# Two of 32 score maxima, the rounding of the maxima and the division of an attention kernel on GpSimd and ScalarE, with value products one step later

## The chip, the cores and the metric

The kernel runs on one core of a Trainium2 chip. The metric is device time in microseconds (us), from launch to end of one execution; lower is better. Engines: PE is TensorE's matmul, PEld its weight load, DVE is VectorE, ACT is ScalarE, POOL is GpSimd, SP is SyncE, which here only issues DMAs.

## What is computed

The program is a stack of four layers on x of shape (1, 2048, 128), all float32. Each layer is a feed-forward half, an attention, and the same feed-forward again; every part adds its result to x.

The four attentions are ordinary softmax attentions:

```
q, k, v = projections of layernorm(x)
s       = q k^T * scale            (per head; layers 0 and 3 causal)
p       = exp(s - rowmax(s))
out     = (p v) / rowsum(p)        (heads joined, output projection, added to x)
```

Layer 0 has 8 heads of 16 and is causal. Layers 1 and 2 have 16 heads of 8 and no mask. Layer 3 has 16 heads of 64 and is causal. The feed-forwards (mixtures of experts, a quantised one, a ternary one) are not touched by the change.

Any number close to the row maximum serves as well as the maximum itself, since it cancels between numerator and denominator; it only has to keep the exponential in range.

## The kernel before

Twelve stages follow one another: ffn0, attn0, ffn0, ffn1, attn1, ffn1 and so on. Stages overlap a little: while one ends, the next takes its first steps where its inputs are ready (the calls of `io.lead`).

The change lies in `flash`, the two-pass attention loop, and in `packed`, which feeds it for attn0, attn1 and attn2. In these, four heads form a group whose rows lie side by side in the partitions, so that four small matmuls run together in the PE array. An iteration `its[n]` is one group `g` and one block `qc` of 512 queries. attn1 and attn2 have four groups and four blocks, 16 iterations each; attn0 has two groups and four blocks.

Every iteration is done twice over its keys.

- Stream A (`stream_a`, `some`, `maxima`) is the first pass. For 128 queries (`r`), 512 keys (`kc`) and two heads (`j0`, `j0 + 1`), PE writes the scores of both heads into one PSUM tile of 2 x 512 columns (line 1071), and VectorE reduces it to two maxima in `mp` (line 1089). A non-causal iteration has 4 x 4 x 2 = 32 such tiles. They live in tag `s1`, which has two buffers. When all are done, `maxima` reduces `mp` over the key blocks to `mx` (line 1100), and `put_max` rounds it into a bf16 part (line 1556) and a bf16 remainder (line 1557) in `top`. Some time later `put` has PE add `top` to the queries by matmuls into `pm` (lines 1566 and 1570), and ScalarE copies that to `q2` (line 1574), so that the scores of the second pass come out with the maximum already subtracted.
- Stream B (`stream_b`) is the second pass. For each 128 keys (`kt`, 16 of them in a non-causal iteration) and each of the four heads, PE writes transposed scores of 128 keys x 512 queries into a bank of tag `s2`, which has three buffers (line 1213), and ScalarE takes the exponential into a tile `pt` (line 1222). `values` multiplies the four `pt` of a `kt` with v and adds them up in `pv`, of which there is one buffer (line 1159); it does so in two halves of the columns, one behind the second head and one behind the fourth head of the next `kt`.

After the last `kt`, `finish` has ScalarE copy `pv` to `ov` (line 1582). A little later `normal` has PE transpose it into an `s2` bank `po` (line 1587), VectorE takes the reciprocal of the row sums (line 1592) and multiplies (line 1593) into `os`. When a block has all its groups, `out_a` and `out_b` project it and add it to x.

PE's order is written out by hand: every matmul of the loop passes through `pe`, which keeps it in program order. The main loop of `flash` interleaves the streams: for the columns that B has emitted it asks how far A should be, runs A up to there, then takes one step of B. In the steady part this gives, per slot, one s2 score, one s1 tile, another s2 score and one half of a value product. Delayed pieces (`put`, `normal`, `out_a`) are queued by `after` with a delay in nanoseconds of an assumed PE clock. VectorE's and ScalarE's orders come from the scheduler, by readiness and priority, with some pairs tied by `in_order`.

In a causal iteration the tile on the diagonal is masked. In attn3 (`halved`), `half_masks` does this with four small bf16 matmuls that add a mask to the scores in PSUM (line 1026). In attn0 (`tiled and causal`) the mask was added by VectorE while it reduced: one `tensor_tensor_reduce` per head with a strip of zeros and minus infinity (line 1081), whose maximum is then read from an accumulator.

Of the kernel before, what the change touches and what calls it, by code (L numbers as in the profile page):

```python
# [17 lines left out]
P = 128  # L18
# [46 lines left out]
def tile_macaron(ctx: ExitStack, tc: tile.TileContext, a: dict, out: bass.AP, stages=STAGES):  # L65
# [32 lines left out]
    minus_half = const.tile([P, TC], F32, name="minus_half")  # L98
    nc.gpsimd.memset(minus_half, -0.5)

    def cs(name):
# [866 lines left out]
    OUT_A = 4000.0  # L968

    def flash(io, pool, early, its, nh, causal, scale, s1, s2, pv_mm, put_max, begin, finish, poll=None,
# [7 lines left out]

        halved = nh == 2
        clock = [0.0]
        total = [0]
        later = []
# [20 lines left out]

        if halved:

            halves = {}  # L1010
            for name in ("ident", "maskq", "maskk"):
                raw = pool().tile([P, 2, P], F32, name="halfraw", tag="halfraw", bufs=2)
                for j in range(2):
                    nc.sync.dma_start(
                        out=raw[P // 2 * j : P // 2 * (j + 1)],
                        in_=a["consts"][:, slice(*CONSTS[name])].rearrange("(b i) k -> i b k", b=2),
                    )
                halves[name] = pool().tile([P, 2, P], BF16, name="half" + name)
                nc.vector.tensor_copy(halves[name], raw)

        def half_masks(outs, mask):

            for b in range(2):
                for j in range(2):
# [3 lines left out]
                    ))  # L1028

        if tiled and causal:  # L1030
            junk = pool().tile([P, CH], F32, name="junk")
            strip = pool().tile([P, CH], F32, name="strip")
            nc.gpsimd.memset(strip[:, : CH - P], 0.0)
            nc.vector.tensor_copy(strip[:, CH - P :], cs("maskq"))

# [18 lines left out]
        def some(n, turns, mp):  # L1054

            g, qc = its[n]
            nk = chunks(qc)
            for first, (r, kcs) in enumerate(turns):
                before = hook(n, kcs[0], r) if hook is not None else None
                if first == 0 and before is None:  # L1060
                    before = newest[0]
                for kc in kcs:
                    for j0 in range(0, nh, 2):
                        ps = first_pass_bank()
                        last = causal and kc == qc
                        masked = last and not tiled
                        w = (r + 1) * P if last else CH
                        for j in range(2):
                            o = j * CH
                            lhsT, rhs = s1(n, j0 + j, r, kc)  # L1070
                            pe(nc.tensor.matmul(  # L1071
                                ps[:, o : o + w], lhsT, rhs[:, :w], start=True, stop=not masked
                            ))
                            pos[0] += w
                        if masked:
                            half_masks([ps[:, j * CH + w - P : j * CH + w] for j in range(2)], "maskq")
                        both = ps.rearrange("p (j n) -> p j n", j=2)
                        with tc.high_priority() if not waiting[0] else nullcontext():
                            if last and tiled:
                                for j in range(2):  # L1080
                                    ins = nc.vector.tensor_tensor_reduce(
                                        junk[:, :w], both[:, j, :w], strip[:, CH - w :], 1.0, NEG,
                                        ALU.add, ALU.max, mp[:, r, j0 + j, kc : kc + 1],
                                    )
                                    if before is not None:
                                        in_order(ins, before)
                                        before = None
                            else:
                                ins = nc.vector.tensor_reduce(  # L1089
                                    mp[:, r, j0 : j0 + 2, kc], both[:, :, :w], AX.X, ALU.max,  # L1090
                                )
                        if before is not None:
                            in_order(ins, before)
                            before = None
                        yield 2 * w if tiled else w

        def maxima(n, mp):
            nk = chunks(its[n][1])
            mx = pool().tile([P, TC, nh], F32, name="mx", tag="mxa", bufs=3)
            nc.vector.tensor_reduce(mx, mp[:, :, :, :nk], AX.X, ALU.max, negate=True)  # L1100
            put, newest[0] = put_max(n, mx, pe)

            def done():
                put()
                ready.add(n)

            after(2000.0, done)

        newest = [None]
        waiting = [False]  # L1110

# [15 lines left out]
        def stream_b():  # L1127
            pend = [None]

            def values(half=None):  # L1130

                if pend[0] is None:
                    return
                n, kt, nt, c0, pts, pv, last_exp = pend[0]
                if halved:
# [12 lines left out]
                if half == 0:  # L1148
                    pend_half[0] = 1
                    if hi == CH:  # L1150
                        pend[0] = None
                        pend_half[0] = 0
                else:
                    pend[0] = None
                for j in reversed(range(nh)):
# [21 lines left out]
            for n, (g, qc) in enumerate(its):  # L1177
# [3 lines left out]
                nt = chunks(qc) * TC  # L1181
                pv = None
                for kt in range(nt):
# [4 lines left out]
                    if halved:  # L1188
# [11 lines left out]
                        for j in range(2):  # L1200
                            pts[j] = early.tile([P, CH], F32, name="pt", tag="pt", bufs=2 * nh + 2)
                            ex = nc.scalar.activation(pts[j][:, c0:], outs[j][:, c0:], AF.Exp, scale=scale)  # L1202
                        step((CH - c0) * (len(terms[0]) - 2))
                        yield 2 * (CH - c0)
                        values()
                    for at_j, j in enumerate(() if halved else order):
                        if alive[0] or at_j % 2:
                            ps = bank("s2")
# [8 lines left out]
                        if diag and not tiled:  # L1217
                            pe(nc.tensor.matmul(
                                ps[:, c0 : c0 + P], masks_b["ident_b"], masks_b["maskk_b"], start=False, stop=True
                            ))  # L1220
                        pt = early.tile([P, CH], F32, name="pt", tag="pt", bufs=2 * nh + 2)
                        ex = nc.scalar.activation(pt[:, c0:], ps[:, c0:], AF.Exp, scale=scale)  # L1222
# [11 lines left out]
                        if tiled and alive[0]:  # L1234
                            if at_j % 2:
                                values(at_j // 2)
                        elif at_j == (split_at if alive[0] else nh - 1):
                            values()
                    if pv is None:
                        pv = held("pv")  # L1240
                    pend[0] = (n, kt, nt, c0, pts, pv, ex)
                    if not alive[0]:
                        io.lead(2.3)
                if poll is not None:
                    at[1] = nt
                    if flush and n + 1 < len(its) and its[n + 1][0] != g:
                        values()
                    poll(at)
            values()

# [70 lines left out]

    def attention_scratch(early):
        return lambda dt, name: early.tile([P, CH], dt, name=name, tag="pt", bufs=10)

    def packed(io, early, hd, causal, scale, project, w, wv, wo, bias=None, outs=True):
# [11 lines left out]
        wv, wo = w[:, wv : wv + C], w[:, wo : wo + C]  # L1337
        scratch = attention_scratch(early)
        vall = [early.tile([P, TC, C], F32, name=f"vall{c}") for c in range(NC)]
# [210 lines left out]

        def put_max(n, mx, pe):
            top = tops[n % 3]
            tv = top.rearrange("p a r (j s) -> p a r j s", s=span)[:, :, :, :, 3:8:4]
            for i in range(nq):
                m = mx[:, :, i * per : (i + 1) * per]
                nc.vector.tensor_copy(tv[:, i, :, :, 0], m)
                last = nc.vector.tensor_tensor(
                    tv[:, i, :, :, 1], m, tv[:, i, :, :, 0], ALU.subtract
                )

# [18 lines left out]
        def finish(n, pv, after, pe):  # L1579
# [4 lines left out]
            def normal():  # L1584
                ps = bank("po")
                for r in range(TC):
                    pe(nc.tensor.transpose(
                        ps[:, r * P : (r + 1) * P], ov[:, r * P : (r + 1) * P], ident
                    ))
                po = ps.rearrange("p (r j m) -> p r j m", r=TC, j=4)  # L1590
                rc = room[0].tile([P, TC, 4], F32, name="rc", tag="rc", bufs=2)
                nc.vector.reciprocal(rc, po[:, :, :, hd])
                nc.vector.tensor_tensor(
                    os[qc][:, :, g * 4 * hd : (g + 1) * 4 * hd].rearrange(
                        "p r (j d) -> p r j d", j=4
                    ),
                    po[:, :, :, :hd],
                    rc.unsqueeze(3).to_broadcast([P, TC, 4, hd]),
                    ALU.mult,
                )  # L1600
                if g == n_groups - 1:
                    after(OUT_A if causal else 1500.0, out_a)
# [61 lines left out]
        with tc.tile_pool(name="att", bufs=1) as pool, tc.tile_pool(name="far", bufs=1) as far:  # L1664
# [10 lines left out]
            room.append(pool)  # L1675
            room.append(far if causal else early if outs else pool)

# [712 lines left out]
```

## Time and profile before

| quantity | value |
|---|---|
| median of three runs | 3737.1 us (3736.11 to 3738.52) |
| the profiled execution, its own time | 3720.81 us |
| its span, first to last instruction | 3719.1 us |
| mean granted TensorE clock | 0.950 |
| busy in the span: PE, PEld | 3404.5 us (92%), 1837.3 us (49%) |
| DVE, ACT, POOL | 2853.9 us (77%), 2025.6 us (54%), 817.1 us (22%) |
| attn0, attn1, attn2, attn3, about | 178 to 450, 790 to 1490, 1650 to 2390, 2580 to 3540 us |
| line 1089, all forms | 1440 reduces, 1627.7 us busy |
| line 1222, all forms | 2368 exponentials, 1220.5 us busy |

How to read the profile: it is one execution, recorded by the hardware. A row of groups has the source line, the engine, the operation, the tiles written and read by their names in the program, their shapes, the count, then busy time in us, the mean of one in ns, and the idle time of the engine just before, with what ended it (`<-`). A row of the timeline has start and duration in us; `x7` are seven such instructions back to back, and a bracket is idle time before it. In a row of stretches, each engine has its busy us and its count of instructions. Durations of back-to-back instructions overlap a little, so a pitch, start to start, is the better measure of what one costs its engine. The tiles of both passes appear as `s`.

The times differ between stages: the shares over the whole span say little about attn1 and attn2, where VectorE and PE are busy 97% and more of most stretches.

### The profile page before, as it was taken

The numbers are of one execution on the slowest core, as the hardware profiler recorded it, in microseconds if no ns is written. First come the engines' busy times: TensorE is split into PE (matmuls) and PEld (weight loads), VectorE is DVE, ScalarE is ACT, GpSimd is POOL, SyncE is SP. The second block draws the span as 40 slices with busy tenths as digits, with TensorE's granted clock in tenths as the row PEclk, the third lists the DMA queues.
The fourth block names the chain that finished last, engine by engine and source line by source line (L and its number), as shares of the span: only waits on it lengthen the run. The fifth ranks groups of instructions, "written<-read, shape, count | busy, mean of one in ns | idle before, by whom it ended". The sixth has DMA issues, their size and how long they took to land. (4 is left out here: it accounts for less than half of the span.)

```text
span 3719.1 us, 64518 instructions
## 1 busy us (share of the span) xinstructions
PE 3404.5 (92%) x25325; PEld 1837.3 (49%) x25325; DVE 2853.9 (77%) x4729; ACT 2025.6 (54%) x3815; POOL 817.1 (22%) x816
## 2 busy tenths in 40 slices
PE   7689987989999999997999999898889999999989
PEld 5543366854333333883333333376444444445457
DVE  6588556778999995778999999544777877788852
ACT  3346722317888888333888888731333344444442
POOL 1511124000000000210000000232555445533341
PEclk9779989979999999996999999898999999999999
DMA  3420123000000000100000000012443232211010
GB/s 106 98 52 14 37 62 91 7 20 9 15 6 16 6 4 7 55 25 21 10 16 10 12 6 1 26 44 68 151 146 112 96 106 98 97 57 52 24 35 12
DMA packets 124977, 170.18 MB, mean 46 GB/s; under 512 B 25152, under 2 KB 52930, under 8 KB 124672
## 3 DMA queue, kind: packets, MB, share of 16 engines
q1 hardware_dynamic: 122112, 160.80, 13.8%
q0 software_dynamic: 2560, 5.25, 0.9%
q8 instruction: 199, 3.26, 0.4%
q14 instruction: 106, 0.87, 0.1%
HBM read 101.25 MB, written 45.87 MB: 40 GB/s over the span
## 5 line engine op out<-in xcount | busy, mean ns | idle before, releaser
L1089 DVE TENSOR_REDUCE mp<-s 128x2 f32<-128x1024 f32 (+3 forms) x1440 | 1627.7, 1183 | 80.2 <-PE s L1071 56.7
L1222 ACT ACTIVATE pt<-s 128x512 f32<-128x512 f32 (+1 forms) x2368 | 1220.5, 601 | 217.7 <-PE s L1213 165.2
L1213 PE MATMUL s<-q,km 32*128 32x512 f32 (+2 forms) x2368 | 735.0, 493 | 28.8 <-ACT pt L1222 18.6
L1159 PE MATMUL pv<-pt,v 128*32 128x256 f32 (+1 forms) x8568 | 732.2, 414 | 22.9 <-ACT ov L1582 11.2
L1071 PE MATMUL s<-km,qt 32*128 32x512 f32 (+3 forms) x2368 | 617.1, 506 | 64.9 <-DVE mp L1089 45.3
L1213 PEld LDWEIGHTS s<-q,km 32*128 32x128 f32 (+1 forms) x2368 | 323.9, 184 | 531.4 <-issue 339.5
L1202 ACT ACTIVATE pt<-s 128x512 f32<-128x512 f32 (+3 forms) x640 | 306.3, 530 | 361.3 <-PE s L1194 216.3
L143 POOL TENSOR_TENSOR rs<-rs,minus_half 128x4 f32<-128x4 f32 x56 | 57.3, 1023 | 1491.8 <-DVE rs L142 1468.1
L2071 DVE TENSOR_TENSOR sum<-sum,pt 128x512 f32<-128x512 f32 (+3 forms) x328 | 260.0, 808 | 86.9 <-ACT pt L1202 85.6
L1159 PEld LDWEIGHTS pv<-pt,v 128*32 128x32 f32 x8568 | 169.2, 108 | 317.7 <-issue 147.1
L1194 PE MATMUL s<-q,k 64*128 64x512 f32 (+3 forms) x1920 | 295.1, 400 | 14.9 <-ACT pt L1202 10.5
L1159 PE MATMUL pv<-pt,latv 128*64 128x512 f32 (+3 forms) x1280 | 307.5, 560 | 1.3 <-ACT pt L1202 1.3
L2071 POOL TENSOR_TENSOR sum<-sum,pt 128x512 f32<-128x512 f32 (+1 forms) x200 | 264.7, 1324 | 179.8 <-ACT pt L1202 176.4
L1071 PEld LDWEIGHTS s<-km,qt 32*128 32x128 f32 (+1 forms) x2368 | 236.2, 191 | 123.8 <-DVE mp L1089 82.3
L1194 PEld LDWEIGHTS s<-q,k 64*128 64x128 f32 x1920 | 159.1, 186 | 222.8 <-issue 140.5
L715 ACT ACTIVATE sg<-pg 128x1024 f32<-128x1024 f32 x72 | 74.0, 1027 | 158.2 <-PE pg L229 142.0
L1071 PE MATMUL s<-k,q 64*128 64x512 f32 (+3 forms) x640 | 131.9, 430 | 19.0 <-DVE mp L1089 18.8
L1873 DVE TENSOR_TENSOR rot<-rot,tab 128x512 f32<-128x512 f32 x128 | 87.8, 686 | 74.8 <-PE rot L229 43.3
L725 PEld LDWEIGHTS pd<-l1d,h 128*128 128x128 f32 x1152 | 139.0, 191 | 5.6
L725 PE MATMUL pd<-l1d,h 128*128 128x128 f32 x1152 | 139.8, 275 | 0.0
L717 DVE TENSOR_TENSOR h<-pu,sg 128x1024 f32<-128x1024 f32 x72 | 87.8, 1220 | 51.7 <-PE pu L229 46.5
L1888 ACT CAST h<-rot 128x512 fp32r<-128x512 f32 x64 | 39.6, 619 | 159.5 <-POOL rot L1883 159.5
(572 smaller groups left out, 4736.3 us busy)
## 6 DMA issues: line engine op xcount, KB each, us to landing
tab<-in_l3rope SPq DMA_DIRECT2D x66, 256.0 KB
q<-q SPq DMA_DIRECT2D x32, 512.0 KB
k<-k SPq DMA_DIRECT2D x32, 512.0 KB
l0e<-in_l0e SPq DMA_DIRECT2D x32, 256.0 KB
q<-h SPq DMA_DIRECT2D x32, 256.0 KB
q<-rot SPq DMA_DIRECT2D x32, 256.0 KB
k<-h SPq DMA_DIRECT2D x32, 256.0 KB
k<-rot SPq DMA_DIRECT2D x32, 256.0 KB
```

Source lines behind the costliest of these rows:

```text
L715: nc.scalar.activation(sg, pg, AF.Silu)
L717: nc.vector.tensor_tensor(h.rearrange("p m n -> p (m n)"), pu, sg, ALU.mult)
L725: nc.tensor.matmul(pd[:, i, :], h[:, m, i * P : (i + 1) * P], wd[:, m, :], start=m == 0, stop=m == 1,)
L1071: pe(nc.tensor.matmul(ps[:, o : o + w], lhsT, rhs[:, :w], start=True, stop=not masked))
L1089: ins = nc.vector.tensor_reduce(mp[:, r, j0 : j0 + 2, kc], both[:, :, :w], AX.X, ALU.max,)
L1159: i = pe(nc.tensor.matmul(pv[out_rows, lo:hi], lhsT, pts[j][:, lo:hi], start=kt == 0, stop=kt == nt - 1 and hi == CH))
L1194: pe(nc.tensor.matmul(outs[j][:, c0:], lhsT, rhs[:, c0:], start=i == 0, stop=i == len(terms[0]) - 1 and not diag,))
L1202: ex = nc.scalar.activation(pts[j][:, c0:], outs[j][:, c0:], AF.Exp, scale=scale)
L1213: pe(nc.tensor.matmul(ps[:, c0:], lhsT, rhs[:, c0:], start=i == 0, stop=i == len(terms) - 1 and (tiled or not diag),))
L1222: ex = nc.scalar.activation(pt[:, c0:], ps[:, c0:], AF.Exp, scale=scale)
L1873: nc.vector.tensor_tensor(t.bitcast(F32), ps, halves["tabs"][i], ALU.mult)
L2071: eng.tensor_tensor(t[:, c0:], other[:, c0:], pts[j][:, c0:], ALU.add)
```

## The change

The edits of `flash` and `packed`:

1. Two tiles aside. In attn1 and attn2 (`aside`), in every iteration but the first, the first-pass tiles (r, kc, j0) = (1, 0, 0) and (1, 2, 2), which are numbers 4 and 21 of 32 (counted from 0), are not reduced by VectorE. `halving` has ScalarE copy the tile to SBUF in two copies of 128 x 512, and GpSimd halve it three times: difference of two halves, maximum with zero, plus the second half. What is left, 2 x 64 columns, is reduced by VectorE in `maxima`, ordered behind the iteration's last plain reduce and ahead of `mx`.
2. Rounding. In the same iterations `put_max` runs its copy and subtraction on GpSimd, and `put` is due 3000 instead of 2000 behind them.
3. Division. In attn1 and attn2, but for the last iteration of each, `normal` has ScalarE copy `po` to `ot`, and GpSimd take the power -1 of the row sums and multiply.
4. Later values. In attn1 and attn2 (`lag`), `pend` is a list, and while stream A lives a value product is emitted half a `kt` later than before: its first half behind the fourth head of the next `kt`, its second half behind the second head of the one after. `pt` has 12 buffers instead of 10.
5. Causal masks. attn0 now masks by `half_masks` like attn3, and reduces masked tiles with the plain reduce; the strip and `tensor_tensor_reduce` are gone. `half_masks` needs two mask tables, loaded by four DMAs at the start of attn0.
6. `ov`, `ot` and `oT` of attn1 lie in another pool.

Counts of instructions, before and after: VectorE 128 masked reduces and 128 accumulator reads to none, plain reduces from PSUM 1440 to 1444, 60 small reduces of what GpSimd left, reciprocals of `po` 40 to 10, and 30 fewer each of the rounding's copy and subtraction and of the multiply in attn1 and attn2. ScalarE 150 more copies. GpSimd 660 more operations. PE 256 more mask matmuls, each with a weight load of its own.

```diff
+    ASIDE = ((1, 0, 0), (1, 2, 2))
...
+        lag = tiled and not causal
...
+        aside = tiled and not causal
...
-                        masked = last and not tiled
+                        masked = last
...
+                        if aside and n and (r, kc, j0) in ASIDE:
+                            halving(ps, mp[:, r, j0 : j0 + 2, kc])
+                            yield 2 * w
+                            continue
                         with tc.high_priority() if not waiting[0] else nullcontext():
-                            if last and tiled:
-                                for j in range(2):
-                                    ins = nc.vector.tensor_tensor_reduce(
-                                        junk[:, :w], both[:, j, :w], strip[:, CH - w :], 1.0, NEG,
-                                        ALU.add, ALU.max, mp[:, r, j0 + j, kc : kc + 1],
-                                    )
...
+                            ins = nc.vector.tensor_reduce(
+                                mp[:, r, j0 : j0 + 2, kc], both[:, :, :w], AX.X, ALU.max,
+                            )
+                            last_max[0] = ins
...
+        def halving(ps, out):
+
+            t = pool().tile([P, 2, CH], F32, name="copied", tag="copied", bufs=2)
+            d = pool().tile([P, 2, CH // 2], F32, name="over", tag="over", bufs=1)
+            for j in range(2):
+                nc.scalar.copy(t[:, j], ps[:, j * CH : (j + 1) * CH])
+            m = CH // 2
+            while m >= CH // 8:
+                nc.gpsimd.tensor_tensor(d[:, :, :m], t[:, :, :m], t[:, :, m : 2 * m], ALU.subtract)
+                nc.gpsimd.tensor_scalar_max(d[:, :, :m], d[:, :, :m], 0.0)
+                nc.gpsimd.tensor_tensor(t[:, :, :m], d[:, :, :m], t[:, :, m : 2 * m], ALU.add)
+                m //= 2
+            left.append((out, t[:, :, : 2 * m]))
...
         def maxima(n, mp):
             nk = chunks(its[n][1])
+            while left:
+                out, t = left.pop(0)
+                in_order(nc.vector.tensor_reduce(out, t, AX.X, ALU.max), last_max[0])
...
+            if aside and n:
+
+                put, _ = put_max(n, mx, pe, nc.gpsimd)
+            else:
+                put, newest[0] = put_max(n, mx, pe)
...
-            after(2000.0, done)
+            after(3000.0 if aside and n else 2000.0, done)
...
                         if tiled and alive[0]:
-                            if at_j % 2:
-                                values(at_j // 2)
+                            if at_j % 2 and (not lag or at_j == nh - 1 or len(pend) > 1):
+                                values(pend_half[0] if lag else at_j // 2)
...
+                if causal or n == len(its) - 1:
...
+                else:
+                    ot = room[1].tile([P, CH], F32, name="ot", tag="ov", bufs=2)
+                    nc.scalar.copy(ot, ps)
+                    po = ot.rearrange("p (r j m) -> p r j m", r=TC, j=4)
+                    rc = room[0].tile([P, TC, 4], F32, name="rc", tag="rc", bufs=2)
+                    nc.gpsimd.tensor_tensor(rc, po[:, :, :, hd], minus_one, ALU.pow)
+                    nc.gpsimd.tensor_tensor(
+                        out, po[:, :, :, :hd],
+                        rc.unsqueeze(3).to_broadcast([P, TC, 4, hd]), ALU.mult,
+                    )
```

## The prediction

> **What bounds the kernel now.** I read the page's 40 slices first, then the busy time of each engine by stretches of 100 us, then the groups, the waits and the timeline inside one attention stage. The slices show two long level stretches, 850 to 1440 and 1750 to 2350 us, the non-causal attentions attn1 and attn2, where nearly all of the change lies. From the stretches (us; then busy us of PE, PEld, DVE, ACT, POOL; granted clock):
>
> ```profile
> 1100.00:1200.00 100.00, 97.56 (x995) 37.49 (x987) 97.91 (x100) 88.35 (x171) 0.00 (x0) 1.00 0.05 13
> 1200.00:1300.00 100.00, 97.60 (x998) 37.76 (x994) 97.52 (x96) 88.51 (x172) 0.00 (x0) 1.00 0.03 8
> ```
>
> VectorE is full, GpSimd empty, ScalarE at 88%. VectorE's groups in 900 to 1350 us:
>
> ```profile
> L1089 DVE TENSOR_REDUCE mp<-s 128x2 f32<-128x1024 f32 x372 | 427.4, 1220 | 3.2 <-PE s L1071 1.7 <-PE s L1213 1.3
> L1593 DVE TENSOR_TENSOR o<-po,rc 128x128 f32<-128x128 f32 x11 | 3.2, 291 | 0.4
> L1592 DVE RECIPROCAL rc<-po 128x16 f32<-128x16 f32 x11 | 2.8, 255 | 5.5 <-PE po L1587 5.5
> L1557 DVE TENSOR_TENSOR top<-mx,top 128x16 bf16<-128x16 f32 x11 | 2.5, 232 | 0.4
> ```
>
> The maxima are nearly all of it. Starts of the mx reduce give an iteration: (1352.55 - 886.12)/12 = 38.87 us for 32 maxima, 64 exponentials and 64 value products. The timeline gives the rules by which one slot (two scores for the second pass, one tile of 2x512 first-pass scores, one eight-matmul value group) passes the engines:
>
> ```profile
> 1099.94 12.73 DVE L1089 TENSOR_REDUCE mp<-s 128x2 f32<-128x1024 f32 x11
> ...
> 1104.56 2.07 ACT L1222 ACTIVATE pt<-s 128x512 f32<-128x512 f32 x4 [0.23 <-PE s L1213]
> ...
> 1105.20 0.49 PE L1213 MATMUL s<-q,km 32*128 32x512 f32 x1
> 1105.69 0.16 PEld L1159 LDWEIGHTS pv<-pt,v 128*32 128x32 f32 x8 [0.31 <-ACT pt L1222]
> ...
> 1106.26 0.50 PE L1213 MATMUL s<-q,km 32*128 32x512 f32 x1
> 1106.27 0.50 PE L1071 MATMUL s<-km,qt 32*128 32x512 f32 x2
> ```
>
> VectorE's pitch is (12.73 - 0.08)/11 = 1.150 here; elsewhere seven take 8.01, 1.133 each. So this pattern is not VectorE alone: the value group waits for the exponential of the slot just before, and the loop score, exponential, value group, score closes in 2.30, two pitches. Four exponentials take 2.07: 0.59 for the last, a pitch of 0.49. A score is read 0.58 to 0.59 after its start; its bank is rewritten 0.64 after its exponential starts (1104.56 to 1105.20). A reduce frees its bank 1.27 after its start (1368.91 to 1370.18). From the second score of a slot to its value group is 0.43 (1122.79 and 1122.98, then 1123.41), the group 0.57. PE needs 1.00 per slot, ScalarE 0.98, VectorE 1.13: all three are close.
>
> Once an iteration PE itself is late:
>
> ```profile
> 1126.59 0.59 ACT L1582 COPY ov<-pv 128x512 f32<-128x512 f32 x1
> ...
> 1127.23 1.06 PE L1159 MATMUL pv<-pt,v 128*32 128x512 f32 x8 [0.47 <-ACT ov L1582]
> 1128.23 0.66 PE L1587 MATMUL po<-cst,ov 128*128 128x128 f32 x4
> ...
> 1128.92 0.26 DVE L1592 RECIPROCAL rc<-po 128x16 f32<-128x16 f32 x1 [0.72 <-PE po L1587]
> 1129.21 0.29 DVE L1593 TENSOR_TENSOR o<-po,rc 128x128 f32<-128x128 f32 x1
> ...
> 1129.42 8.03 DVE L1089 TENSOR_REDUCE mp<-s 128x2 f32<-128x1024 f32 x7
> ```
>
> The score of that reduce starts at 1128.82, behind the transposes; plus 0.58 is 1129.40. The reciprocal and multiply sit inside PE's delay.
>
> **Parts with little on the path** (30 of the 32 non-causal iterations carry the new code).
> - Division to ScalarE copy and GpSimd: VectorE loses 0.55, gain 0, since the reduce behind it waits for PE anyway. po's bank, which the multiply held until PE's 1129.65, is now held by the copy: transposes end about 1128.89, +0.59 +0.05 = 1129.5. The GpSimd power has only the 128x4 row (1.02); 128x16 lies between 1.0 and four times that, off the path.
> - Rounding to GpSimd: VectorE's pause at the boundary is 1120.19 - 1119.47 = 0.72; cast and subtract are about 0.48 of it. In their place come two end reductions over 2x64, about 0.2 each (the 2x512 one has 1.13, the 128x64 one 0.22). Gain 0.1. GpSimd's two small operations, between 0.2 and 1.0 each (power row), reach PE's pm matmul, moved a slot later, 1.0 early or 0.4 late; I take early.
> - Later values: the 2.30 loop is cut, so 23 slots go from 1.150 to 1.133: gain 0.4.
>
> **The two tiles moved aside.** The sum that speaks for them: VectorE loses 2 x 1.13 + 0.48 + 0.55 - 0.40 = 2.9 of an iteration. [...] The row speaks otherwise: first-pass scores have only two banks. With bank A given to ScalarE, the next tile must go to B, free 1.27 after its reduce began, and is readable 0.58 later: VectorE idles 1.85 - 1.13 = 0.72. So at best an aside saves 1.13 - 0.72 = 0.41, less 0.2 for its end reduction.
>
> Against that stands ScalarE. The built order puts both copies between the slot's first and second exponential (x, copy, copy, y). In a stretch paced by VectorE, time 0 at the start of reduce k-1, tile k aside (x at 0.02, its tile at 0.14): x exponential 0.61, copies 1.10 and 1.59, y 2.08, so y's bank is free at 2.72. Next slot's tile to B at 1.27, its reduce 1.85 (free at 2.98), its value group ends 2.27. Slot k+2 needs y's bank: 2.72, its reduce 3.30, its second score waits for ScalarE until 3.21, value group ends 4.21. Slot k+3: reduce 4.79. Slot k+4: reduce 5.92. Undisturbed it would begin at 5 x 1.13 = 5.65. So the second aside (tile 21) costs 0.27 although a reduce is gone: three score banks cannot hold a 0.98 backlog.
>
> The first aside (tile 4) comes just behind ScalarE's q copy and ahead of the ov/po delay. The same rules, from reduce 31 at 0 with end reductions and mx to 1.80: reduces 0 to 3 at 1.80, 2.93, 4.07, 5.33 (PE delayed 0.67 by pm); copies at 6.83 and 7.33; reduces 5, 6, 7 at 7.56, 9.04, 10.53; ov copied by 10.91, value group and transposes to 12.50, reduce 8 at 13.08. Before, reduce 31 began at 1118.34 and reduce 8 at 1129.42 + 1.15: 12.23. So +0.85; with the 0.4 gained by later values and 0.27 for the second aside, +0.7 per iteration, x 30 = +21 us. Without asides the same walk has reduce 8 at 11.96: -0.66 in all, so two asides cost 1.4.
>
> **GpSimd beside VectorE.** [...] In attn3:
>
> ```profile
> 3308.75 1.27 POOL L2071 TENSOR_TENSOR sum<-sum,pt 128x512 f32<-128x512 f32 x1 [1.11 <-ACT pt L1202]
> 3309.13 1.45 DVE L2071 TENSOR_TENSOR sum<-sum,pt 128x512 f32<-128x512 f32 x1 [0.37 <-ACT pt L1202]
> ...
> 3321.14 2.36 DVE L1089 TENSOR_REDUCE mp<-s 128x2 f32<-128x1024 f32 x2 [0.29 <-PE s L1071]
> 3321.58 1.27 POOL L2071 TENSOR_TENSOR sum<-sum,pt 128x512 f32<-128x512 f32 x1 [1.29 <-ACT pt L1202]
> ```
>
> An add of two operands doubles beside GpSimd (0.68 alone), two reduces from PSUM keep 2.36. [...] I take 0. GpSimd's own time: per tile 2 x 1.27 + 0.71, then 256 and 128 wide, about 6.5 by the slope between 1.27 (512) and 1.00 (384). Tile 21 leaves ten slots, 11.3, less 2.2 for ScalarE: 9 available.
>
> **The causal masks (attn0).** 128 masked reduces with accumulator reads (62 + 11 us by rows of 0.69, 0.56, 0.42, 0.28 and 0.08) become 64 plain ones of 1.22, 0.94, 0.68, 0.41, 16 each: 52. VectorE loses 21. PE gains 256 small matmuls; in attn3 four take 0.09 (3315.51 to 3315.60) to 0.28, so 6 to 18 us. PE's waits for L1081 sum to 36.8. Ends: -20 and +6; I take -9, since early attn0 is paced by those reduces. The mask loads are four DMAs on SP's queue between y loads, well ahead of the km and qt transfers; 0. The ov tile's other pool: 0.
>
> **Sum.** +21 - 9 = +12 us on the profiled 3720.8 (span 3719.1 plus 1.7), 3733. That execution is 16.3 below the median of 3737.1, so the median becomes 3749.
>
> **Rivals.**
> 1. Faster: ScalarE absorbs the copies. Its idle in 900 to 1350 us is 53 us, 4.6 an iteration, against 2.5 added. If the copies do not reach PE through y's bank, the walk without asides holds: -0.66 x 30 - 9 = -29, 3708. It decides from 0.33 us per aside downward. For: the idle time; against: only 0.15 of it lies in each slot. Chance 0.30.
> 2. Nothing visible: asides cost 1.0, not 1.4: +0.3 x 30 - 9 = 0, 3737. Chance 0.20.
> 3. GpSimd late: tiles need over 9 us, or the small operations 1 us each, and VectorE or PE waits 0.4 to 1 more: +12 to +30 on top, 3769. Chance 0.13.
> 4. The forecast, 3749. Chance 0.37.
>
> The measurement tells about 0.2% (7.5 us) from no change: faster 0.30, same 0.20, slower 0.50. Range 3709 to 3774: just short of rival 1's best end, and into rival 3.
>
> **What would show it.** Iterations (mx to mx) of about 39.6 instead of 38.9; VectorE's idle before the reduce behind each aside 0.7 or more, and again in the next two slots; PE's second-pass scores waiting for ScalarE there; plain slots at 1.13; reduces still 1.22 long beside GpSimd; attn0 some 9 shorter. I am wrong if slots around tiles 4 and 21 keep 1.13, or if the end reductions wait for GpSimd.

## The result

The changed kernel takes 3855.05 us (median of 6 runs, 3819.29 to 3884.92) against 3736.61 us before (6 runs, 3727.35 to 3750.81): 1.0299 times the time before, 95% interval 1.0275 to 1.0324. The profiled execution is the slowest of the six, 1.7% above the fastest; the ratio is of the other five, whose median is 3844.74. The change is slower, as forecast, but by 118 us (108 by those five) where 12 were forecast, and it lies outside the range.

### The profile page after: what moved, and what is told of

The parts are those of the page before. It is cut to its first block, busy times and chain, and to the rows that moved or that the text cites. A ratio compares the mean times of both kernels' runs of the same rounds, so it can differ in the third digit from the quotient of the medians.

```text
span 3883.1 us, 65216 instructions
## 1 busy us (share of the span) xinstructions
PE 3516.5 (91%) x25581; PEld 1867.2 (48%) x25581; DVE 2784.6 (72%) x4418; ACT 2107.3 (54%) x3965; POOL 1398.6 (36%) x1476
## 5 line engine op out<-in xcount | busy, mean ns | idle before, releaser
L1248 ACT ACTIVATE pt<-s 128x512 f32<-128x512 f32 (+1 forms) x2368 | 1238.0, 606 | 242.9 <-PE s L1239 194.2
L1239 PE MATMUL s<-q,km 32*128 32x512 f32 (+2 forms) x2368 | 781.1, 532 | 47.3 <-ACT pt L1248 37.6
L1183 PE MATMUL pv<-pt,v 128*32 128x256 f32 (+1 forms) x8568 | 799.2, 449 | 20.3 <-ACT ov L1607 11.2
L1073 PE MATMUL s<-km,qt 32*128 32x512 f32 (+3 forms) x2368 | 659.0, 542 | 59.9 <-DVE mp L1085 56.9
L1104 POOL TENSOR_TENSOR over<-copied 128x512 f32<-128x512 f32 x180 | 147.5, 819 | 598.8 <-ACT copied L1101 589.9
L1073 PEld LDWEIGHTS s<-km,qt 32*128 32x128 f32 (+1 forms) x2368 | 250.8, 204 | 118.8 <-DVE mp L1085 106.2
L1105 POOL TENSOR_SCALAR over<-over 128x512 f32<-128x512 f32 x180 | 171.8, 954 | 15.6
L1106 POOL TENSOR_TENSOR copied<-over,copied 128x512 f32<-128x512 f32 x180 | 148.2, 823 | 14.5
L1917 POOL TENSOR_TENSOR rot<-rot,rot 128x512 f32<-128x512 f32 x64 | 90.1, 1408 | 162.1 <-DVE rot L1907 155.0
```

The lines of the kernel that those rows point to most:

```text
L1073: pe(nc.tensor.matmul(ps[:, o : o + w], lhsT, rhs[:, :w], start=True, stop=not masked))
L1104: nc.gpsimd.tensor_tensor(d[:, :, :m], t[:, :, :m], t[:, :, m : 2 * m], ALU.subtract)
L1105: nc.gpsimd.tensor_scalar_max(d[:, :, :m], d[:, :, :m], 0.0)
L1106: nc.gpsimd.tensor_tensor(t[:, :, :m], d[:, :, :m], t[:, :, m : 2 * m], ALU.add)
L1183: i = pe(nc.tensor.matmul(pv[out_rows, lo:hi], lhsT, pts[j][:, lo:hi], start=kt == 0, stop=kt == nt - 1 and hi == CH))
L1239: pe(nc.tensor.matmul(ps[:, c0:], lhsT, rhs[:, c0:], start=i == 0, stop=i == len(terms) - 1 and (tiled or not diag),))
```

## The profile after

The profiled execution has a span of 3883.1 us, its own time is 3884.92 us. The row of TensorE's granted clock over the span, first before, then after:

```profile
PEclk9779989979999999996999999898999999999999
```

```profile
PE   7699878979999998997899998879889999999999
DVE  6488456678678877488789887654567777788862
PEclk9789989979578978997899898889899999999999
```

Slices 10 to 16 are attn1 and 20 to 26 are attn2. PE stays full there, VectorE reads mostly six to nine, and the clock has a five, sevens and eights where it had nines. The mean clock is 0.910 instead of 0.950. Its loss, (1 - clock) times time, grows from 186 to 348 us over the span: in attn1 (first to last mx reduce) from 7.5 to 113, in attn2 from 10 to 62. The other runs say the same: the fastest, 3819 us, had 0.935, while the kernel before had 0.941 to 0.952 in its runs beside the first experiments.

The two stretches that the prediction began with, now:

```profile
1100.00:1200.00 100.00, 97.17 (x858) 34.45 (x854) 79.98 (x76) 82.72 (x159) 42.41 (x47) 0.81 0.03 9
1200.00:1300.00 100.00, 95.59 (x887) 35.08 (x879) 83.57 (x81) 85.06 (x163) 43.26 (x53) 0.88 0.03 9
```

In the first stretch PE shows the same 97 us of busy time for 858 matmuls instead of 995: each is longer (0.113 us of it a matmul instead of 0.098). VectorE's groups in 900 to 1350 us:

```profile
L1085 DVE TENSOR_REDUCE mp<-s 128x2 f32<-128x1024 f32 x303 | 356.9, 1221 | 84.9 <-PE s L1239 69.9 <-PE s L1073 14.6
L1114 DVE TENSOR_REDUCE mp<-copied 128x2 f32<-128x128 f32 x20 | 4.7, 278 | 0.0
```

A reduce is as long as before (1221 ns against 1220), with GpSimd busy for 42 to 43 us of each of the two stretches beside it. Its idle time went from 3.2 to 84.9 us, and PE's scores end it.

The timeline behind one first aside shows the forecast walk (the prediction's step-by-step timing of one iteration) and, at its end, what was not forecast (the mx reduce of this iteration begins at 969.75):

```profile
974.86 1.07 ACT L1101 COPY copied<-s 128x512 f32<-128x512 f32 x2
...
975.59 1.23 DVE L1085 TENSOR_REDUCE mp<-s 128x2 f32<-128x1024 f32 x1 [0.95 <-PE s L1239]
...
976.48 0.49 PE L1239 MATMUL s<-q,km 32*128 32x512 f32 x1 [0.39 <-ACT pt L1248]
...
977.05 1.23 DVE L1085 TENSOR_REDUCE mp<-s 128x2 f32<-128x1024 f32 x1 [0.24 <-PE s L1073]
...
978.53 1.23 DVE L1085 TENSOR_REDUCE mp<-s 128x2 f32<-128x1024 f32 x1 [0.25 <-PE s L1239]
...
978.92 1.52 PE L1183 MATMUL pv<-pt,v 128*32 128x512 f32 x8 [0.45 <-ACT ov L1607]
...
980.38 1.12 PE L1612 MATMUL po<-cst,ov 128*128 128x128 f32 x4
...
981.42 0.79 PE L1239 MATMUL s<-q,km 32*128 32x512 f32 x1
```

The reduces behind the aside follow at 1.46 and 1.48 (975.59, 977.05, then 978.53), where the walk had 1.48 and 1.49. But the value product then takes 1.52 instead of 1.06, the transposes 1.12 instead of 0.66, a score 0.79 instead of 0.50. The stretches there give the clock:

```profile
978.00:979.00 1.00, 0.55 (x12) 0.23 (x12) 0.75 (x2) 1.00 (x3) 0.92 (x2) 1.00 0.00 0
979.00:980.00 1.00, 1.00 (x8) 0.08 (x8) 0.76 (x1) 0.86 (x2) 1.00 (x1) 0.70 0.00 0
980.00:981.00 1.00, 1.00 (x7) 0.63 (x4) 0.00 (x0) 0.00 (x0) 0.92 (x2) 0.50 0.00 0
...
985.00:990.00 5.00, 5.00 (x40) 1.34 (x36) 3.47 (x3) 3.24 (x6) 2.73 (x2) 0.50 0.14 37
```

From 979.4 the clock is half, until 1027.2. At half clock the usual slot is 1.74 us instead of 1.13 (median pitch of the reduces), and PE reads fully busy. An iteration with a long stretch of this kind takes 49 to 57 us. Inside a group of heads, most iterations at full clock take 39.20 to 39.25 us, against 38.5 to 38.7 before.

## The theories

A: the asides and the later values leave places where TensorE's array has little to do; the granted clock falls there and stays low for a while. B: the work of GpSimd and ScalarE draws the clock down. C: the later values or the new order do, whatever the asides. D: the clock wanders by itself.

For A the array's work was added up from the timeline of each run. Each matmul counts with its share of 128 rows x 128 columns, the largest weights in the traces (`128*128`), times its streamed columns, with 0.43 us for a full 128x512 one (start to start in the run with the extra matmuls, 1312.60 to 1313.03). It is an estimate from the records. Busy time does not show this: before, four 32-row scores start within 0.01 us at 1106.26, each 0.49 to 0.50 long; behind the first aside one starts alone at 976.97, also 0.49 long, and shows as just as busy.

## The experiments

All ratios are to the kernel before, run beside each version on the same chip. The kernel before took 3733.2 to 3738.3 us (medians) in these sets of runs, so a difference between medians of two sets is good to some 5 us. "Inner" iterations are those from mx reduce 2 to 12 of attn1 and 18 to 28 of attn2 (attn1 has mx reduces 0 to 15, attn2 16 to 31), 22 in each profile; the group of heads changes at every multiple of 4.

**No asides.** `ASIDE = ()`.

> The changed kernel with every maximum left on VectorE: no tile is set aside, all else stays (later values, GpSimd's rounding and division, attn0's masks). Theory A (the asides make TensorE wait, and its waits bring the granted clock down in attn1 and attn2): no stretch of half clock in attn1 and attn2, iterations near 37.9 to 38.2 us at full clock, 3695 to 3720 us. Rival B (the work of GpSimd and ScalarE draws the clock down): the division and rounding stay, so part of the half-clock stretches should stay; 3740 to 3800. Rival C (the later values or the new order take TensorE's clock): the stretches stay as they are, 3800 to 3850. Rival D (the clock wanders whatever the kernel): dips as often as before, 3780 to 3850.

Measured: 3751.42 us, ratio 1.0043 (1.0022 to 1.0064). That is 31 us above A's range. Iterations take 37.9 us, the walk without asides. But among the inner iterations three half-clock stretches of 10 to 27 us are left, each at a change of the group of heads (mx reduces 4, 20 and 24). And in the last group PE stands before the output projection:

```profile
1368.41 2.91 POOL L1630 TENSOR_TENSOR rc<-ot,minus_one 128x16 f32<-128x16 f32 x1 [9.85 <-ACT ot L1627]
...
1371.40 0.41 POOL L1631 TENSOR_TENSOR o<-ot,rc 128x128 f32<-128x128 f32 x1
1371.86 1.12 PE L1641 MATMUL oT<-cst,o 128*128 128x128 f32 x4 [2.48 <-POOL o L1631]
...
1374.79 1.23 DVE L1085 TENSOR_REDUCE mp<-s 128x2 f32<-128x1024 f32 x1 [4.27 <-PE s L1239]
```

The power and the multiply end 3.5 us behind the copy of `po` (1368.34 to 1371.81); the output transposes, due 1500 ns behind, stand at the head of PE's queue, all scores behind them, and VectorE loses 4.27 us. The clock halves there too, for 3.4 us. A alone did not name this; the asides are not the whole cause.

**Values at their old place, asides kept.** `lag = False`, `pt` keeps 12 buffers.

> The changed kernel with the value products at their old place (no lag; the twelve pt buffers stay), the asides kept. Theory A: the asides still make TensorE wait, the half-clock stretches stay, iterations 39.2 to 39.8 us at full clock, 3830 to 3890 us. Rival C (the later values bring the clock down): full clock in attn1 and attn2, 3745 to 3765.

Measured: 3857.45 us, ratio 1.0315 (1.0277 to 1.0354). Half-clock stretches stay, so the later values are not needed for them, and C falls as the main cause. In this profile they begin at five of the six changes of group and in none of the other inner iterations. At full clock an iteration takes 40.6, not 39.2 to 39.8 as expected: beside asides the later values are worth 1.4.

**GpSimd busy, nothing aside.** `halving` works on a fixed tile; the output does not use it. ScalarE's copies are left out.

> As the run with no aside, but GpSimd does the halving work of the two asides (nine operations each) on a fixed SBUF tile, begun when VectorE's reduce of tile 4 or 21 has ended; nothing reads its result, no ScalarE copy is added and the outputs are unchanged. Theory A: GpSimd's work costs neither clock nor path: within 5 us of the run with no aside. Rival B (GpSimd's work draws the clock down or slows VectorE's reduces from PSUM): half-clock stretches in attn1 and attn2, 30 to 120 us more than the run with no aside.

Measured: 3784.47 us, ratio 1.0137 (1.0104 to 1.017): 33 us over no asides, where A gave under 5. Yet inner iterations stay at 37.9, VectorE's reduce has 1215 ns in both runs, and only 2 of 22 inner iterations begin a half-clock stretch, both at a change of group. The excess lies at the ends of attn1 and attn2: attn1's iterations 13 and 14 take 53.6 and 53.8 us (47.9 and 46.8 without), since the division now stands behind a halving:

```profile
1379.25 1.12 PE L1646 MATMUL oT<-cst,o 128*128 128x128 f32 x4 [6.41 <-POOL o L1636]
```

So the number is B's, but B's mechanism is not seen: GpSimd's queue is a cost of its own. ScalarE's share of B is left to the runs with the array filled, below.

**The asides alone on the kernel before.**

> The kernel before with the asides alone: tiles 4 and 21 of iterations 1 to 15 go by ScalarE's copies and GpSimd's halving; values, rounding, division and attn0's masks stay as before. Theory A: about 1.4 us more for each of 30 iterations at full clock (40 us), and half-clock stretches on top: 3830 to 3900 us. Rival C: no half-clock stretches, 3765 to 3785. Rival D: whatever the clock does, no tie to the asides.

Measured: 3829.39 us, ratio 1.0246 (1.021 to 1.0282), 0.6 us under A's range. Iterations at full clock take 40.4, 1.85 more than before, where 1.4 was expected. Six of 22 inner iterations begin a stretch, 8.1 to 9.2 us behind mx, beside the value product and the transposes, as in the changed kernel (9.3 to 10.6 us). None of the other edits is in this kernel: the asides alone bring the stretches.

**Last group's division back on VectorE** (no asides).

```diff
-                if causal or n == len(its) - 1:
+                if causal or g == n_groups - 1:
```

> As the run with no aside, but the last group of heads (iterations 12 to 15) has its division on VectorE straight from PSUM again. Theory A2 (in those iterations the output transposes stand on TensorE's queue for GpSimd's division, 2.5 to 2.8 us of wait and a half-clock stretch of 4 to 11 us each, three times in each attention, and some 7 us in the step behind the last iteration): 20 to 30 us less than the run with no aside, so 3722 to 3731 us; iterations 13 and 14 back near 44 and 43 us. Rival (the tail is longer for the later values or the later rounding): within 6 us of the run with no aside.

Measured: 3731.04 us, ratio 0.9978 (0.9962 to 0.9994): 20.4 us less, though of another set of runs (24 by the ratios). Attn1's iterations 13 and 14 take 43.8 and 42.8 us. The division in the last group is confirmed.

**No drain at a change of group** (and the edit above). With the drain, the loop emits all value products still pending at the end of a group at once; without it they follow as inside a group.

```diff
-                    if flush and n + 1 < len(its) and its[n + 1][0] != g:
+                    if flush and not lag and n + 1 < len(its) and its[n + 1][0] != g:
```

> The run before, and the later values are not drained at the end of each group of heads. Theory A (the granted clock falls where TensorE's array has little to do for about 3.4 us: with no aside that is only behind the change of group, where the drained products leave 1.38 us of full-array work in the emptiest 3.4 us against 2.0 in the other iterations): no half-clock stretch of over 10 us at 8 to 10 us behind a maximum, all inner iterations at 37.9 to 38.0 us; 25 to 40 us less than the run before it, 3688 to 3705 us. Rival (the stretches come from elsewhere: GpSimd, or chance): the stretches stay, 3715 to 3735 us.

Measured: 3702.69 us, ratio 0.9902 (0.9883 to 0.9921), better than both kernels. So the later values do cost clock, where they are drained. No inner iteration loses clock:

```profile
1100.00:1200.00 100.00, 97.84 (x1019) 39.74 (x1014) 96.81 (x92) 93.04 (x175) 8.18 (x10) 1.00 0.05 13
1200.00:1300.00 100.00, 97.71 (x1019) 39.30 (x1015) 96.20 (x88) 93.55 (x178) 10.97 (x10) 1.00 0.03 7
```

**More work for the array beside the asides.** In the changed kernel, with `s1.whole` the same operands over all 128 rows:

```diff
+                        if aside and n and (r, kc, j0) in ((1, 0, 2), (1, 1, 2)):
+                            lhsT, rhs = s1.whole(n, r, kc)
+                            pe(nc.tensor.matmul(ps[:, :CH], lhsT, rhs, start=True, stop=True))
...
```

> The changed kernel with more work: ahead of the scores of tiles 5 and 7 TensorE does one matmul of all 128 rows by 512 columns (about 0.43 us each) into the same bank, which the scores then overwrite; 60 of them, 26 us of TensorE's time, and no result changes. Theory A (too little work in the array takes the clock): the emptiest 3.4 us behind a maximum has over 2.0 us of full-array work instead of 1.66, the half-clock stretches that begin there go except at a change of group, and more work gives less time: 3790 to 3825 us. Rival B (the draw of the other engines, or of the array itself, takes the clock) and rival D (chance): the stretches stay or grow, 3860 to 3890 us.

Measured: 3835.71 us, ratio 1.0249 (1.0226 to 1.0272): 26 us more matmul work, 19 us less time (9 by the changed kernel's five; the intervals of the two ratios barely part, so the stretches are the clearer sign). Outside changes of group no inner iteration begins a stretch any more, though ScalarE's copies and GpSimd's work are all there, so B falls; all six changes of group begin one. The time is eleven us above A's range and well below the rivals'.

**The same matmuls elsewhere**, ahead of tiles (3, 0, 0) and (3, 1, 0), numbers 12 and 14.

> The changed kernel with the same 60 full-array matmuls of 0.43 us, but ahead of tiles 12 and 14, some 17 to 20 us behind a maximum, where the array is full. Theory A (the place decides): nothing gained, the half-clock stretches stay where they were, and up to 0.6 us more per iteration: 3855 to 3885 us. Rival (any more matmul work keeps the clock up): as with the matmuls ahead of tiles 5 and 7, 3825 to 3845 us.

Measured: 3889.41 us, ratio 1.0431 (1.0404 to 1.0458), 54 us more than at the empty place and 4 above A's range. Iterations at full clock take 40.6 to 40.9 instead of 39.5 to 39.8, some 33 us of the 54 (1.4 over the changed kernel's 39.2, where I allowed 0.6). Stretches stay: six inner iterations begin one, five of them at a change of group. The place decides.

**Both asides, division and drain mended.** The last group's division is on VectorE and there is no drain, as in the two runs above.

> The changed kernel with its two asides, but with the last group's division on VectorE and no drain at a change of group. Theory A: at full clock 1.3 us more per iteration than the run without drain and aside (40 us in all), and half-clock stretches of 20 to 45 us stay behind some of the asides, since the emptiest 3.4 us still has 1.66 us of work: 3760 to 3810 us. Were the drain and the division the whole cause of the lost clock: 3730 to 3745 us.

Measured: 3770.65 us, ratio 1.008 (1.005 to 1.0111), from 3750 to 3807 as the clock goes from 0.948 to 0.927. The two mends take 84 us off the changed kernel (74 off its five), and the asides still cost 68 over none; 39 are the walk, 30 times 39.2 - 37.9.

**The same with the array filled** beside the asides.

> Both asides, last group's division on VectorE, no drain at a change of group, and the 60 full-array matmuls ahead of tiles 5 and 7. Theory A: no emptiest 3.4 us under 1.9 us of full-array work is left in the inner iterations, so no half-clock stretch there; 0.3 us more per iteration at full clock than without the matmuls, yet less time: 3740 to 3758 us against 3771, and a spread of under 20 us against 57. Rival D (chance): 3770 to 3800 us.

Measured: 3774.76 us, ratio 1.0106 (1.009 to 1.0123). The spread was 10 us in four runs (57 in nine without the matmuls) and no inner iteration begins a stretch behind mx. But nothing is saved, and the time is 17 us above A's range: a miss, which the runs on iterations 3 to 12 below take up.

**Tile 21 alone aside**, all mended. `ASIDE = ((1, 2, 2),)`

> The mended kernel without asides (last group's division on VectorE, no drain at a change of group), and tile 21 alone set aside, tile 4 not. Theory A (an aside takes the clock only where it lies beside the copy and the transposes of the finished products, 6 to 9 us behind a maximum; tile 21's lies near 26 us): 0.2 to 0.4 us more per iteration at full clock, no half-clock stretch of over 10 us in the inner iterations: 3706 to 3718 us against 3703 without any aside. Rival B (each aside's copies and GpSimd work take the clock, wherever it lies): half of the loss of both, with stretches behind tile 21: 3730 to 3745 us.

Measured: 3733.98 us, ratio 1.0002 (0.9987 to 1.0016): B's number. But no inner iteration begins a stretch, and they take 38.2 to 38.3, +0.33. Attn2's first iterations hold most of the excess (57.0, 50.9 and 42.3 us, without it 53.2, 40.3 and 37.8):

```profile
1827.33 0.45 POOL L1106 TENSOR_TENSOR copied<-over,copied 128x128 f32<-128x128 f32 x1
1827.74 1.26 POOL L1805 TENSOR_TENSOR rot<-rot,rot 128x512 f32<-128x512 f32 x1
...
1829.03 0.62 ACT L1386 CAST qH<-rot 128x512 fp32r<-128x512 f32 x1 [4.58 <-POOL rot L1805]
...
1830.20 0.79 PE L1239 MATMUL s<-q,km 32*128 32x512 f32 x1 [4.41 <-ACT pt L1248]
```

A rotation that belongs to the query and key preparation stands on GpSimd's queue behind the halving; ScalarE's cast waits for it with the exponentials behind, PE waits 4.41 us, and the clock is half for the next 20.5.

**Two runs again, in iterations 3 to 12 only:** tile 21 alone, and both asides with the array filled. `if aside and 2 < n < 13 ...`

> As the run with tile 21 alone set aside, but in iterations 3 to 12 only. Theory A3 (the excess comes from other stages' GpSimd operations standing behind a halving in iterations 1, 2 and 13 to 15): 20 asides at 0.33 us, 7 us over the run without asides, 3703 to 3716 us. Rival (each aside takes clock wherever it lies): two thirds of the excess stays, 3720 to 3728 us.

> As the run with both asides, the mended drain and division and the full-array matmuls ahead of tiles 5 and 7, but asides and matmuls in iterations 3 to 12 only. Theory A3: what is left is the walk at full clock, 20 iterations at 39.6 instead of 37.95 us, 33 us over the run without asides: 3728 to 3745 us. Rival (asides cost clock even with the array filled): 3750 us or more.

Measured: 3705.3 us, ratio 0.9905 (0.9872 to 0.9937), and 3735.01 us, ratio 0.9992 (0.9976 to 1.0009). Both lie in the ranges of the theory that other stages' GpSimd operations wait behind a halving at the ends. In these profiles no inner iteration loses clock: where no such operation is queued behind, and tile 4 is not aside or the array is filled beside it, asides cost their walk and no clock.

**Rounding and division all on VectorE**, no asides, no drain.

> The mended kernel without asides, and rounding and division all on VectorE as before (the due time of the rounding too): of the change there stay the later values and attn0's masks. Theory A (VectorE's own work sets the iteration, and GpSimd takes 0.43 us of rounding and 0.5 us of division from it, of which the stall behind the transposes hides most): 0.1 to 0.5 us more per iteration, 3705 to 3720 us. Rival (GpSimd's division and rounding are the whole gain of the iteration): 38.5 us per iteration, 3722 us or more. Were the later values the whole gain: 3695 to 3704 us.

Measured: 3704.64 us, ratio 0.9923 (0.9905 to 0.9941). The time lies between two of the ranges, so the iterations decide: they take 37.9 us, as with GpSimd. The later values are the whole gain of the iteration.

## What takes the clock

The inner iterations (mx reduces 2 to 12 and 18 to 28) of all 16 profiled executions, by the array's work in its emptiest 3.4 us, the shortest half-clock stretch inside the profiles, between 1 us before and 13 us behind mx (read where the clock held); "began" are iterations in which the clock falls, 8 to 11 us behind mx:

| full-array work in 3.4 us | where | iterations | began |
|---|---|---|---|
| 1.86 to 2.24 | before, inside a group; no asides; asides with the array filled; tile 21 alone; four changes of group without drain | 214 | 0 |
| 1.77 | before, change of group | 6 | 0 |
| 1.56 to 1.67 | both asides | 79 | 9 |
| 1.36 to 1.42 | no asides, drained at a change of group | 18 | 8 |
| 0.83 to 0.98 | asides at a drained change of group | 24 | 19 |

Six changes of group (the array filled, still drained) all fell, so their work could not be read; they and five iterations that began at half clock are left out. Shown: the fewer full-array us in the window, the oftener the clock falls (in 0 of 220 iterations from 1.77 up, 9 of 79 at 1.56 to 1.67, 8 of 18 at 1.36 to 1.42, 19 of 24 under 1); filling or emptying the place switches it. Busy time does not order them: before, PE's least busy 3.5 us have 2.54 to 2.73 us, without asides 2.73 to 2.81, and only the latter falls.

The table takes the emptiest 3.4 us wherever they lie. The clock records of the traces say where to look. In each of the 16 profiles every change of the clock lies on one grid with a step of 3.413 us, to within 1 ns (65 changes in the profile before, 97 in the one after), and the stretches last whole steps: 3.4, 6.8, 10.2 us and so on, up to 47.8 in the profile after. When the work is counted in the steps of that grid, for the same iterations and where the clock was full in the step and in the one before, the cases part well (the bounds are read from the data):

| full-array work in one step of the grid | steps | half clock from its end |
|---|---|---|
| under 1.62 us | 24 | 24 |
| 1.62 to 1.85 us | 66 | 18 |
| above 1.85 us | 3719 | 0 |

So D falls too, and most of what looks like chance inside a row of the first table is where the borders of the grid happen to lie. The kernel before kept its clock in part by luck: its lowest step had 1.94 us, but its changes of group have an emptiest 3.4 us of 1.77.

Not shown: how the clock follows from this work. The falls need no long wait of PE: in the steps before these 42 falls its longest wait was 0.98 us (0.39 and 0.45 in the timeline above). The transposes of `po` lie at the place. Counted in full they order the steps better (45 steps that held lie below the fullest one that fell; 188 when they are left out), but no run isolates them.

## Why the prediction was wrong

- **The walk** was right. Forecast per iteration: without asides -0.66, with both +0.7. Measured at full clock inside a group: 37.9 against 38.55, -0.65; 39.2, +0.65. First aside +0.85 forecast, +0.95 measured (39.2 - 38.27); second +0.27, measured +0.33. The +21 us of the sum were about 20.
- **The failed step is the sum**, "+21 - 9 = +12 us": it has no term for the clock. It carried on every duration at 1.00, because the two stretches that it began with showed 1.00. That is a measurement of the old order, not a constant. In its place the runs showed a clock that falls: in the two profiles, whose times are 164 us apart, its loss in attn1 and attn2 together went from 18 to 175 us. What pulled the clock down are the waits for ScalarE, which the walk itself found, and the drain at a change of group, at which it did not look.
- **"Division ... gain 0"** failed for the last group: the power was bounded rightly (2.91 us, between 1.0 and four times that) but called off the path. Its reader there, the output transposes, is due 1500 ns later on PE. This cost 20.4 us.
- **The queue of GpSimd** was checked for the asides' own deadline alone: 9 us available, 6.5 forecast, 8.4 measured from first to last operation (the step with the maximum takes 1.48, not 0.71). It was kept. What else stood behind it in the queue was not looked at: the late aside in the end iterations costs 29 us (3733.98 - 3705.3), of which 3 are the walk of ten asides.
- **Later values**: the gain is real, 0.65 and not 0.4, and rounding on GpSimd gives nothing measurable, not 0.1. But the drain of the later values at a change of group costs 28 us (3731.04 - 3702.69), which the walk of one inner iteration could not see.
- **GpSimd beside VectorE**: 0, right (a reduce has 1221 ns beside it, 1220 before). **attn0**: 218.6 to 205.6 us from first to last mx, -13 against -9; its clock loss fell from 21 to 8 us, so part of that is clock, and no run isolates the masks. The 14 profiles with the new masks have 205.6 to 208.3 us, the two with the old ones 218.6 and 230.7.
- **Rivals.** The first (3708) fell with the copies, which do reach PE through y's bank (`<-ACT pt` at 976.48); its number is near that of the mended kernel without asides. The second put asides at 1.0 an iteration; they cost 1.3. The third had the right engine, but it was the division and other stages' work that came late, not the asides.

The accounts in medians: from the changed kernel, mending division and drain gives -84 (-74 by its five), leaving out the asides -68, and from there to the kernel before +36 (3738.31 - 3702.69): -116 of 118. Of the 84, 49 are seen without asides. The other 35 (25) come only with them; the last row of the first table, 0.83 to 0.98, says why this may be, but no run takes them apart.

## What to carry to other kernels

Where TensorE is near full in many small matmuls, check every edit for the emptiest 3 to 4 us of array work that it leaves, not only for the mean: the granted clock of the old profile holds for the old order (here 1.00 from 1100 to 1200 us before, 0.81 after). Before moving work to an idle engine, list what else is queued on it in every iteration, the first and last ones above all, and who reads the result when. Here the version to keep is the later values without the drain, with no tile aside: 0.9902 (0.9883 to 0.9921); with rounding and division left on VectorE it is as fast (0.9923, 0.9905 to 0.9941).

## What the hardware showed

- The clock goes to 0.50 without a wait of over 1 us on PE (0.44 to 0.47 us inside a group of heads, 0.54 to 0.98 at a change), and stays there for up to 47.8 us in the profile after; in these, from 979.4, PE reads 5.00 busy of 5.00 in every 5 us from 980 to 1025.
- Its changes lie on a grid of 3.413 us in every profile. No step with over 1.85 us of full-array work ended in half clock (3719 steps), and every one with under 1.62 did (24).
- GpSimd on 512 columns of float32: subtract or add 1.27 to 1.28 us, maximum with a constant 1.48; the power on 128x16 2.91.
- VectorE's reduces from PSUM keep 1.22 us beside GpSimd (mean 1221 ns of 303 after, 1220 of 372 before).
